# GpSimd takes 64 columns of each pair's exponential in a graph attention stage

## The chip, the cores and the metric

The kernel runs on one core of a Trainium2 chip. The metric is the device time of one execution in microseconds (us); the time before is the median of three runs. The engines are called PE (TensorE's matrix products; PEld its weight loads), DVE (VectorE), ACT (ScalarE), POOL (GpSimd) and SP (which issues most of the DMAs).

## The reference, cut to what matters

The reference is a graph network of four layers over 3327 nodes with 128 features and a dense 0/1 adjacency matrix. Each layer normalises `x`, applies a ReLU and adds its result to `x`. Nearly all of the time lies in layer 1, an attention in which each of 128 "heads" has only 8 features per node, and the adjacency matrix is added to the scores twice:

```python
q = (x @ Wq.T).reshape(d, n, h)        # d = 128 heads, n = 3327 nodes, h = 8
k = (x @ Wk.T).reshape(d, n, h)
v = (x @ Wv.T).reshape(d, n, h)
a = jnp.einsum('dnh,dmh->dnm', q, k) * scale
a = a + spatial_encoding + edge_encoding      # both are adj
a = jax.nn.softmax(a, axis=2)
out = jnp.einsum('dnm,dmh->dnh', a, v)
```

So for each of the 128 heads an array of 3327 x 3327 scores is made, 2*adj is added, the exponential is taken, and the result weighs the values. There are some 1.4 billion exponentials.

## The kernel before

The query nodes are cut into 7 chunks of columns, six of 476 and one of 471 (rounded up to 472 where an even width is needed). The heads are taken in 32 groups of four, and the 3327 keys in 26 tiles of up to 128. The loops run over chunks, then groups, then key tiles: 7 x 32 x 26 steps. Two neighbouring tiles, an even one and an odd one, make a **pair**, of which there are 7 x 32 x 13 = 2912. A pair has eight arrays of scores (four heads, two tiles) of 128 keys x 476 queries, held in one SBUF buffer `p8` with eight places. There are three such buffers in turn.

The order of the stage is written out by hand (`manual_schedule`); each engine works through its own queue in the order in which the program issues the instructions. A pair goes like this:

- PE makes the four products of the even tile into four PSUM banks `early` (L551), and DVE adds 2*adj (`a2`) to each and writes the sums to places 0 to 3 (L554).
- For the odd tile PE makes three products into a PSUM tile `late` and the fourth into an `early` bank. DVE adds `a2` to the fourth and writes it to place 4: this is the fifth sum of the pair. To one of the three late arrays PE itself adds `a2`, by a product with twice the identity (L570).
- ACT takes the exponential of the three late arrays into places 5 to 7 (L572), and then that of the five sums, in place (L575).
- Two of the late arrays haven't had `a2` added. For them POOL multiplies the exponentials by exp(2*adj), which is kept as `e_a` (L574). Where POOL has other work, this is one array rather than two, and PE adds to two: that is for the first five pairs of the first 30 groups of the first chunk, in which POOL also parts the queries and keys of a coming group into high and low halves (L376, L377).
- The exponentials weigh the values in products that follow four steps, or two pairs, behind (L582); after the last tile DVE copies the result (L591) and it is stored.

Between these, once a pair, a strided copy of two key tiles is made for the next group (`key_pair`, L426): on DVE right after the fifth add, but for one pair in a group on POOL. POOL also doubles the adjacency tiles of the next chunk (`doubled`, L273), 26 of them over the 32 groups of a chunk, and clears one column of `k_in` (L395) in each group.

```python
PLACES = ((0, 1, 2, 3), (5, 6, 7, 4))
...
scores(step, pairs, q4, a_t[t], e_t[t // 2], p8, 1 if parting and t < 10 else 2)
begun[j] = (step, v4, p8)
if j >= ahead:
    weigh(*begun.pop(j - ahead))
```

Of the kernel before, what the change touches and what calls it, by code (L numbers as in the profile page):

```python
# [1 line left out]

# [6 lines left out]
F32 = mybir.dt.float32  # L9
# [6 lines left out]
AF = mybir.ActivationFunctionType  # L16
ALU = mybir.AluOpType
# [4 lines left out]
P = 128  # L22
# [9 lines left out]
QW = 476  # L32
# [5 lines left out]
def rows_of(t):  # L38
    return P if t < T - 1 else P - 1
# [15 lines left out]
def kernel(  # L55
# [23 lines left out]
    nc = tc.nc  # L79

    const = ctx.enter_context(tc.tile_pool(name="const", bufs=1))
# [89 lines left out]
    def load_rows(dst, src, t, col0, w):  # L171

        def part(p0, p1):
            nc.sync.dma_start(dst[p0:p1, :w], dram(src, (p0 * T + t) * N + col0, [[T * N, p1 - p0], [1, w]]))

        if t < T - 1:
            part(0, P)
        else:
            part(0, 112)
            part(112, P - 1)  # L180
# [161 lines left out]
    def even(c):  # L342
        w = q_chunks[c][1]
        return w + w % 2

    def exp_of(a2, c):
        e = e_pool.tile([P, QW], F32, name="e")
        nc.scalar.activation(e[:, : even(c)], a2[:, : even(c)], AF.Exp)
        return e
# [72 lines left out]
    def key_pair(engine, k_in, pairs):  # L422

        t = 2 * len(pairs)
        k = kq.tile([P, 2, P], F32R, name="k", bufs=T // 2 + 2)
        engine.tensor_copy(k, slots(k_in)[:, t : t + 2, :])  # L426
        pairs.append(k)
# [84 lines left out]

    assert T % 2 == 0
    PLACES = ((0, 1, 2, 3), (5, 6, 7, 4))
    two_i = const.tile([P, P], BF16, name="two_i")
    nc.vector.tensor_copy(two_i, ident)
    engines = {
# [9 lines left out]
    with tc.tile_pool(name="at_in", bufs=1) as a_pool, tc.tile_pool(name="at_p", bufs=3) as p_pool, tc.tile_pool(  # L527
        name="at_ps", bufs=1, space=PSUM
    ) as ps:
        acc = ps.tile([P, 512], F32, name="acc")  # L530
        nc.vector.memset(acc, 0.0)

        def load_adj(c, t):

            q0, w = q_chunks[c]
            a = a_pool.tile([P, QW], F32, name="a_in", bufs=1)
            load_rows(a, adjT, t, q0, w)
            return a, t, w

        def store_adj(c, t, a2):  # L540
            q0, w = q_chunks[c]
            nc.sync.dma_start(adj16[t][:, q0 : q0 + w], a2[:, :w])

        def scores(step, pairs, q4, a2, e_a, p8, n_g):
            c, _, t = step
            we = even(c)
            k = pairs[t // 2]

            def product(i, sp, stop=True):
                r = slice(32 * i, 32 * i + 32)  # L550
                nc.tensor.matmul(sp[:, :we], k[r, t % 2, :], q4[r, :we], start=True, stop=stop)  # L551

            def add(i, sp):
                nc.vector.tensor_tensor(p8[:, PLACES[t % 2][i], :we], sp[:, :we], a2[:, :we], op=ALU.add)  # L554

            if t % 2 == 0:
                early = [ps.tile([P, 512], F32, name="early", bufs=4) for _ in range(4)]
                for i in range(4):
                    product(i, early[i])
                for i in range(4):  # L560
                    add(i, early[i])
                return
            n_i = 3 - n_g
            late = ps.tile([P, 3, 512], F32, name="late")
            early = ps.tile([P, 512], F32, name="early", bufs=4)
            for i in range(3):
                product(i, late[:, i], stop=i >= n_i)
            product(3, early)
            for i in range(n_i):
                nc.tensor.matmul(late[:, i, :we], two_i, a2[:, :we], start=False, stop=True)  # L570
            add(3, early)
            nc.scalar.activation(p8[:, 5:8, :we], late[:, :, :we], AF.Exp)  # L572
            g8 = p8[:, 8 - n_g : 8, :we]
            nc.gpsimd.tensor_tensor(g8, g8, e_a[:, :we].unsqueeze(1).to_broadcast([P, n_g, we]), op=ALU.mult)  # L574
            nc.scalar.activation(p8[:, :5, :we], p8[:, :5, :we], AF.Exp)  # L575

        def weigh(step, v4, p8):
            c, g, t = step
            q0, w = q_chunks[c]
            kp = rows_of(t)  # L580
            for i in range(4):
                nc.tensor.matmul(  # L582
                    acc[32 * i : 32 * i + EA, :w],
                    v4[:kp, i, t, :],
                    p8[:kp, PLACES[t % 2][i], :w],
                    start=(t == 0),
                    stop=(t == T - 1),
                )
            if t == T - 1:
                o4 = a_pool.tile([P, QW], F32, name="o4")  # L590
                nc.vector.tensor_copy(o4[: 96 + EA, :w], acc[: 96 + EA, :w])  # L591
                for i in range(4):
                    n0 = (4 * g + i) * N + q0
                    nc.sync.dma_start(ot[:, n0 : n0 + w], o4[32 * i : 32 * i + EA, :w])

        with tc.manual_schedule(engines=engines):
            groups = [(c, g) for c in range(len(q_chunks)) for g in range(n_groups)]
            steps = [(c, g, t) for c, g in groups for t in range(T)]
            (q4, v4), pairs = first, k_first
            a_t, a_next = a_first, []  # L600
            e_t, e_next = e_first, []
            to_store = [(0, t, a2) for t, a2 in enumerate(a_t)]
            begun = {}
            for j, step in enumerate(steps):
                c, g, t = step
                n = c * n_groups + g + 1
                more = n < len(groups)
                if t == 0:
                    if j:
                        (q4, v4), pairs = coming, k_coming  # L610
                        if g == 0:
                            a_t, a_next = a_next, []
                            e_t, e_next = e_next, []
                    k_coming = []
                if t % 2 == 0:
                    p8 = p_pool.tile([P, 8, QW], F32, name="p8")
                parting = c == 0 and g + 2 < n_groups
                scores(step, pairs, q4, a_t[t], e_t[t // 2], p8, 1 if parting and t < 10 else 2)
                begun[j] = (step, v4, p8)
                if j >= ahead:  # L620
                    weigh(*begun.pop(j - ahead))
                if t == 4 and more:
                    coming = load_rest(*groups[n])
                if parting:
                    if t == 0:
                        part = ahead_part
                    for due in range(t, t + 1 if t < T - 1 else max(T, 16)):
                        part.at(due)
                        if due == 15 and g + 3 < n_groups:
                            ahead_part = Parting(g + 3)  # L630
                            ahead_part.load(0)
                            ahead_part.load(1)

                if t % 2 and more:
                    key_pair(nc.gpsimd if t == ahead - 1 else nc.vector, k_ins[n], k_coming)
                if t == 14 and n + 1 < len(groups):
                    k_ins.append(load_keys(groups[n + 1][1]))
                if t == min(6, T // 2) and c + 1 < len(q_chunks):
                    for _ in range(min(len(to_store), 1 + T // n_groups)):
                        store_adj(*to_store.pop(0))  # L640
                    a_in = [load_adj(c + 1, i) for i in range(len(a_next), T * (g + 1) // n_groups)]
                if t == max(T - 4, 3) and c + 1 < len(q_chunks):
                    for a, i, w in a_in:
                        a_next.append(doubled(adj_pools[(c + 1) % 2], a[: rows_of(i), :w], i, w))
                        to_store.append((c + 1, i, a_next[-1]))
                if t % 2 and g == n_groups - 1 and c + 1 < len(q_chunks):
                    e_next.append(exp_of(a_next[t], c + 1))
            for j in range(len(steps) - ahead, len(steps)):
                weigh(*begun.pop(j))
            for a in to_store:  # L650
                store_adj(*a)
# [374 lines left out]
    with tc.For_i(0, n_once, 1):  # L1026
# [28 lines left out]
        with tc.tile_pool(name="gb", bufs=2) as pool, tc.tile_pool(name="gb_ps", bufs=2, space=PSUM) as ps, tc.tile_pool(  # L1055
            name="gb_acc", bufs=1, space=PSUM
# [3 lines left out]
            with tc.For_i(0, NH // 4, 1) as g:  # L1060
# [8 lines left out]
                for q0, w in chunks(N, QW):  # L1069
                    q4 = pool.tile([P, QW], F32, name="gq4")  # L1070
# [64 lines left out]
```

## Time and profile before

| | us |
|---|---|
| median of 3 runs | 11047.67 (11043.29 to 11047.72) |
| the profiled execution | 11044.8 |
| its span, first to last instruction | 11043.1 |
| mean granted TensorE clock | 0.988 |
| DVE busy | 10416.8 |
| ACT busy | 10027.8 |
| POOL busy | 7228.9 |

The first exponential of a pair starts at 590 us and the last one ends at 10315 us, so the attention stage has 88% of the span. "Busy" is the time in which at least one instruction of the engine is under way. Instructions of one engine overlap at their ends, so what one adds to its engine's time is the distance from its start to the next one's start, and not its duration. A group line of the profile reads: source line, engine, operation, names of output and inputs, shapes and types, count, then the busy time, the mean ns of one, the idle time before, and what ended it.

### The profile page before, as it was taken

The numbers are of one execution on the slowest core, as the hardware profiler recorded it, in microseconds if no ns is written. First come the engines' busy times: TensorE is split into PE (matmuls) and PEld (weight loads), VectorE is DVE, ScalarE is ACT, GpSimd is POOL, SyncE is SP. The second block draws the span as 40 slices with busy tenths as digits, with TensorE's granted clock in tenths as the row PEclk, the third lists the DMA queues.
The fourth block names the chain that finished last, engine by engine and source line by source line (L and its number), as shares of the span: only waits on it lengthen the run. The fifth ranks groups of instructions, "written<-read, shape, count | busy, mean of one in ns | idle before, by whom it ended". The sixth has DMA issues, their size and how long they took to land. (4 is left out here: it accounts for less than half of the span.)

```text
span 11043.1 us, 201872 instructions
## 1 busy us (share of the span) xinstructions
PE 10674.7 (97%) x76743; PEld 3215.5 (29%) x76768; DVE 10416.8 (94%) x18105; ACT 10027.8 (91%) x6240; POOL 7228.9 (65%) x4288
## 2 busy tenths in 40 slices
PE   9799999999999999999999999999999999999896
PEld 4322222222222222222222222222222222222453
DVE  8599999999999999999999999999999999999656
ACT  0399999999999999999999999999999999999432
POOL 0278887777777777777777777777777766666203
PEclk9899999999999999999999999999999999999998
DMA  7755555333333333333333333333333333333432
GB/s 264 228 142 127 123 124 120 63 67 68 63 70 65 62 71 64 65 69 63 65 71 63 66 69 62 69 65 62 69 64 62 72 58 60 60 56 64 139 106 99
DMA packets 417648, 943.48 MB, mean 85 GB/s; under 512 B 67952, under 2 KB 345953, under 8 KB 380956
## 3 DMA queue, kind: packets, MB, share of 16 engines
q1 hardware_dynamic: 412906, 920.68, 38.9%
q8 instruction: 606, 9.93, 0.4%
q0 software_dynamic: 3760, 9.78, 0.3%
q14 instruction: 376, 3.08, 0.1%
HBM read 790.49 MB, written 139.71 MB: 84 GB/s over the span
## 5 line engine op out<-in xcount | busy, mean ns | idle before, releaser
L554 DVE TENSOR_TENSOR p<-early,a 128x476 f32<-128x476 f32 (+1 forms) x14560 | 8409.7, 645 | 115.7 <-PE early L551 90.1
L574 POOL TENSOR_TENSOR p<-p,e 128x952 f32<-128x952 f32 (+2 forms) x2912 | 6333.2, 2175 | 2690.2 <-ACT p L572 2285.3
L575 ACT ACTIVATE p<-p 128x2380 f32<-128x2380 f32 (+1 forms) x2912 | 7424.2, 2550 | 0.0
L582 PE MATMUL acc<-p,v 128*9 128x476 f32 (+1 forms) x46592 | 5736.5, 564 | 50.8 <-issue 35.0
L572 ACT ACTIVATE p<-late 128x1428 f32<-128x1428 f32 (+1 forms) x2912 | 4998.2, 1716 | 13.9 <-DMA q<-qt 10.3
L551 PE MATMUL early<-q,k 32*128 32x476 f32 (+1 forms) x14560 | 3682.7, 478 | 29.9 <-DVE p L554 7.5
L551 PEld LDWEIGHTS early<-q,k 32*128 32x128 f32 x14560 | 1578.3, 182 | 2725.5 <-DVE p L554 2702.2
L426 DVE CAST k<-k_in 128x256 fp32r<-128x256 f32 x2676 | 1467.7, 548 | 0.0
L551 PE MATMUL late<-q,k 32*128 32x476 f32 (+1 forms) x8736 | 1416.6, 479 | 49.5 <-ACT p L572 49.3
L551 PEld LDWEIGHTS late<-q,k 32*128 32x128 f32 x8736 | 548.5, 182 | 2371.9 <-ACT p L572 2204.6
L570 PE MATMUL late<-a,two_i 128*128 128x476 bf16 (+1 forms) x3062 | 1122.5, 375 | 0.0
L582 PEld LDWEIGHTS acc<-p,v 128*9 128x9 f32 x46592 | 702.1, 89 | 1363.5 <-issue 1288.5
L570 PEld LDWEIGHTS <-two_i 128*128 128x128 bf16 x3062 | 281.3, 96 | 662.7 <-issue 662.7
L190 ACT COPY agg<-agg_ps 128x512 f32<-128x512 f32 x15 | 8.2, 591 | 486.6 <-PE agg_ps L205 290.1
L273 POOL TENSOR_SCALAR a<-a_in 128x476 bf16<-128x476 f32 (+2 forms) x156 | 239.4, 1535 | 0.5
L231 PE MATMUL agg_ps<-a,part 128*128 128x512 bf16 (+1 forms) x1067 | 227.8, 371 | 6.2 <-ACT agg L953 3.2
L273 POOL TENSOR_SCALAR a<-a 128x476 bf16<-128x476 f32 (+1 forms) x26 | 36.4, 1400 | 287.8 <-DMA a<-in_adjT_dram 287.8
L426 POOL CAST k<-k_in 128x256 fp32r<-128x256 f32 x236 | 175.2, 746 | 12.5 <-DMA q<-qt 12.5
L948 PE MATMUL sp<-yT,hT 128*128 128x512 f32 (+1 forms) x364 | 171.3, 612 | 11.6 <-ACT agg L953 5.7
L205 PE MATMUL agg_ps<-a,h 128*128 128x512 f32 (+2 forms) x364 | 147.7, 569 | 26.2 <-DVE h L165 26.2
L591 DVE COPY o<-acc 105x476 f32<-105x476 f32 (+1 forms) x224 | 145.9, 651 | 12.0 <-PE acc L582 7.0
L864 POOL TENSOR_TENSOR xs_late<-xs_late,b_s 128x3328 f32<-128x3328 f32 x1 | 7.3, 7268 | 225.2 <-DVE ln_xc L160 225.2
(239 smaller groups left out, 2860.9 us busy)
## 6 DMA issues: line engine op xcount, KB each, us to landing
k_in<-kt SPq DMA_DIRECT2D x1792, 207.9 KB
v<-vd SPq DMA_DIRECT2D x896, 117.0 KB
a<-in_adjT_dram SPq DMA_DIRECT2D x50, 1663.5 KB
a<-adj SPq DMA_DIRECT2D x78, 831.8 KB
q<-qt SPq DMA_DIRECT2D x1536, 29.8 KB
a_in<-in_adjT_dram SPq DMA_DIRECT2D x125, 238.0 KB
adj<-a SPq DMA_DIRECT2D x156, 119.0 KB
vd<-v_st SPq DMA_DIRECT2D x25, 576.0 KB
```

Of the source, the lines that this page charges most:

```text
L205: nc.tensor.matmul(acc[c][:, :w], lhs[:kp, t, :], a[:kp, c0 : c0 + w], start=(t == 0), stop=(t == T - 1))
L231: nc.tensor.matmul(acc[c][:, :w], part[:, t, :], a[:, c0 : c0 + w], start=(t == 0 and i == 0), stop=(t == T - 1 and i == len(parts) - 1),)
L273: nc.gpsimd.tensor_scalar(a2[:kp, :w], a, 2.0, None, op0=ALU.mult)
L426: engine.tensor_copy(k, slots(k_in)[:, t : t + 2, :])
L551: nc.tensor.matmul(sp[:, :we], k[r, t % 2, :], q4[r, :we], start=True, stop=stop)
L554: nc.vector.tensor_tensor(p8[:, PLACES[t % 2][i], :we], sp[:, :we], a2[:, :we], op=ALU.add)
L570: nc.tensor.matmul(late[:, i, :we], two_i, a2[:, :we], start=False, stop=True)
L572: nc.scalar.activation(p8[:, 5:8, :we], late[:, :, :we], AF.Exp)
L574: nc.gpsimd.tensor_tensor(g8, g8, e_a[:, :we].unsqueeze(1).to_broadcast([P, n_g, we]), op=ALU.mult)
L575: nc.scalar.activation(p8[:, :5, :we], p8[:, :5, :we], AF.Exp)
L582: nc.tensor.matmul(acc[32 * i : 32 * i + EA, :w], v4[:kp, i, t, :], p8[:kp, PLACES[t % 2][i], :w], start=(t == 0), stop=(t == T - 1),)
L948: nc.tensor.matmul(sp[:, c0 : c0 + w], slots(zT)[:, t, :], z2T[:, cols], start=True, stop=False)
```

## The change

In every pair but those in which POOL parts queries and keys, POOL raises e to the last 64 columns of the fifth sum, in place, by a `tensor_tensor` with the operation `pow`, whose first operand is a column of e read for every element. It stands in POOL's queue just ahead of the pair's multiply. ACT's second exponential leaves these 64 columns out: it reads 5 x 476 - 64 = 2316 columns (2296 in the last chunk) rather than 2380 (2360). For that, the places of `p8` now lie next to each other in the last chunk too, with 472 columns each rather than 476.

```diff
+    W_POW = 64
+    base = const.tile([P, 1], F32, name="base")
+    nc.vector.memset(base, math.e)
...
-        def scores(step, pairs, q4, a2, e_a, p8, n_g):
+        def scores(step, pairs, q4, a2, e_a, p8, n_g, w_pow):
...
-            nc.scalar.activation(p8[:, 5:8, :we], late[:, :, :we], AF.Exp)
-            g8 = p8[:, 8 - n_g : 8, :we]
+            nc.scalar.activation(p8[:, 5:8], late[:, :, :we], AF.Exp)
+            flat = p8.rearrange("p i w -> p (i w)")
+            if w_pow:
+                last = flat[:, 5 * we - w_pow : 5 * we]
+                nc.gpsimd.tensor_tensor(last, base.to_broadcast([P, w_pow]), last, op=ALU.pow)
+            g8 = p8[:, 8 - n_g : 8]
             nc.gpsimd.tensor_tensor(g8, g8, e_a[:, :we].unsqueeze(1).to_broadcast([P, n_g, we]), op=ALU.mult)
-            nc.scalar.activation(p8[:, :5, :we], p8[:, :5, :we], AF.Exp)
+            sums = flat[:, : 5 * we - w_pow]
+            nc.scalar.activation(sums, sums, AF.Exp)
...
-                    p8 = p_pool.tile([P, 8, QW], F32, name="p8")
+                    p8 = p_pool.tile([P, 8 * QW], F32, name="p8")[:, : 8 * even(c)].rearrange("p (i w) -> p i w", i=8)
                 parting = c == 0 and g + 2 < n_groups
-                scores(step, pairs, q4, a_t[t], e_t[t // 2], p8, 1 if parting and t < 10 else 2)
+                parts_now = parting and t < 10
+                scores(step, pairs, q4, a_t[t], e_t[t // 2], p8, 1 if parts_now else 2, 0 if parts_now else W_POW)
```

More of the change, by code (lines that the diff above doesn't have):

```diff
@@ L1 @@
+import math
 from contextlib import ExitStack
```

## The prediction

> **What bounds the kernel now.** I read four views: the engine shares, the table of stretches, the costliest groups, and the timelines of ScalarE, GpSimd and VectorE over the same microseconds. The chain that ended last never leaves the final stage here, so it can't name the bound of the attention stage; the table of stretches can. First the shares, then a stretch inside that stage (its columns are PE, weight loads, DVE, ACT, POOL, granted clock, DMA share, GB/s).
>
> ```profile
> PE 10674.7 (97%) x76743; PEld 3215.5 (29%) x76768; DVE 10416.8 (94%) x18105; ACT 10027.8 (91%) x6240; POOL 7228.9 (65%) x4288
> ```
> ```profile
> 5000.00:6400.00 1400.00, 1379.81 (x10480) 377.12 (x10483) 1381.63 (x2515) 1400.00 (x853) 996.91 (x510) 1.00 0.35 67
> ```
>
> ScalarE is busy for all 1400 us; PE and DVE look nearly as full, POOL is at 71%. The groups give the work of one pair of key tiles (2912 pairs): five adds (L554) on DVE, one multiply (L574) on POOL, two exponentials (L572, L575) on ACT.
>
> ```profile
> L554 DVE TENSOR_TENSOR p<-early,a 128x476 f32<-128x476 f32 (+1 forms) x14560 | 8409.7, 645 | 115.7 <-PE early L551 90.1
> L574 POOL TENSOR_TENSOR p<-p,e 128x952 f32<-128x952 f32 (+2 forms) x2912 | 6333.2, 2175 | 2690.2 <-ACT p L572 2285.3
> L575 ACT ACTIVATE p<-p 128x2380 f32<-128x2380 f32 (+1 forms) x2912 | 7424.2, 2550 | 0.0
> L572 ACT ACTIVATE p<-late 128x1428 f32<-128x1428 f32 (+1 forms) x2912 | 4998.2, 1716 | 13.9 <-DMA q<-qt 10.3
> ```
>
> Busy shares hide overlap and stalls, so I use distances between starts. ScalarE's timeline:
>
> ```profile
> 5625.05 2.53 ACT L575 ACTIVATE p<-p 128x2380 f32<-128x2380 f32 x1
> 5627.12 1.70 ACT L572 ACTIVATE p<-late 128x1428 f32<-128x1428 f32 x1
> 5628.36 2.54 ACT L575 ACTIVATE p<-p 128x2380 f32<-128x2380 f32 x1
> 5630.44 1.71 ACT L572 ACTIVATE p<-late 128x1428 f32<-128x1428 f32 x1
> 5631.68 2.54 ACT L575 ACTIVATE p<-p 128x2380 f32<-128x2380 f32 x1
> ```
>
> L575 takes 2.08 us and L572 1.24, 3.32 a pair, without a gap: ScalarE sets the period. The extra columns of L575 cost (2.08 - 1.24)/(2380 - 1428) = 0.88 ns each. Over a whole chunk of columns (416 pairs) the timeline puts the first L572 at 1992.59 and the next chunk's at 3382.29: 3.341 us a pair with everything in it. In the last chunk it is 3.299. Now GpSimd and VectorE, where one doubling (L273) falls:
>
> ```profile
> 5628.90 2.23 POOL L574 TENSOR_TENSOR p<-p,e 128x952 f32<-128x952 f32 x1 [1.10 <-ACT p L572]
> 5631.10 1.57 POOL L273 TENSOR_SCALAR a<-a_in 128x476 bf16<-128x476 f32 x1
> 5632.64 2.22 POOL L574 TENSOR_TENSOR p<-p,e 128x952 f32<-128x952 f32 x1
> 5635.55 2.23 POOL L574 TENSOR_TENSOR p<-p,e 128x952 f32<-128x952 f32 x1 [0.69 <-ACT p L572]
> ```
> ```profile
> 5624.43 0.39 DVE L426 CAST k<-k_in 128x256 fp32r<-128x256 f32 x1
> 5624.74 2.88 DVE L554 TENSOR_TENSOR p<-early,a 128x476 f32<-128x476 f32 x5
> ...
> 5631.32 2.87 DVE L554 TENSOR_TENSOR p<-early,a 128x476 f32<-128x476 f32 x5
> 5634.12 1.01 DVE L426 CAST k<-k_in 128x256 fp32r<-128x256 f32 x1
> 5635.06 1.21 DVE L554 TENSOR_TENSOR p<-early,a 128x476 f32<-128x476 f32 x2
> ```
>
> Two things. Five adds take 2.80 us (5631.32 to 5634.12), a free key cast 0.31; with the copy of a group's results that is 3.15 a pair, so DVE has about 0.17 to spare. And the cast that begins while POOL multiplies lasts until 5635.13, 0.27 after the multiply's end (5634.86): it can't run beside a POOL multiply. The idle 1.10 us of POOL is thus partly the cast's place. The reverse shows in POOL's own casts, 0.42 at the median and up to 0.62 where they come after a held-up DVE cast: 0.20 lost to POOL.
>
> ```profile
> L376 POOL CAST hi<-lo_q x128: 404/419/624, 395.5 to 1874.3; 96x278 fp32r<-96x278 f32 x96, 96x275 fp32r<-96x275 f32 x32
> L395 POOL MEMSET k_in<- 128x1 f32 x224 | 22.9, 103 | 0.0
> ```
>
> **The change, part by part.** The power runs wherever POOL has no parting work: 2912 pairs less 5 in each of 30 groups, 2762.
>
> *ScalarE, less.* 64 columns x 0.88 ns = 56 ns, times 2762 = 155 us, all of it on the path as long as ScalarE sets the period. The Trainium skill ("ScalarE: Activation LUTs", Rules for kernel authors) calls ScalarE the only option for an exponential; by that rule nothing would be moved, and the sum would be the time of before.
>
> *Next late.* DVE at 3.15 and PE, whose pair takes 3.10 where nothing holds it (early products start at 5002.62 and 5005.72), are both under the new 3.27, so neither takes the 56 ns away while casts stay free.
>
> *GpSimd, more: the unknown.* No row shows a power. From below: the two-input multiply, (2230 - 1205)/476 = 2.15 ns a column between its 952- and 476-column forms and 0.18 us fixed, so 0.18 + 64 x 2.15 ns = 0.32 us; nothing can be below that row by much, since the power too reads two operands and writes one, and a negative cost is excluded because an instruction is added to POOL and none taken away. From above: a power is a logarithm and an exponential. With a cubic for each (three multiply-adds), a step that splits off the exponent and one that puts it back, I count ten operations beyond what a multiply does, and twice that for a careful version. One operation costs at most a whole one-input pass: the cast row, (0.419 - 0.103)/277 = 1.14 ns a column with its read and write, 0.073 us for 64. Ten make 0.32 + 0.73 = 1.05 us, twenty 1.78. Between 0.32 and 1.78 I take 1.05: by what it computes the power is nearer to a chain of passes than to one multiply. By the Trainium skill ("GPSIMD Engine Reference", section 3.1), loop bodies of three or more operations run about three a cycle at 1.2 GHz; ten would add about 0.18 us, the power would be an estimated 0.50 us and the change would gain; no trace here shows that rate.
>
> *The new wait.* The power waits for DVE's fifth add, and stands ahead of the same pair's multiply in POOL's queue; behind it are that multiply, a key cast per group, the doubling and the memset of k_in. DVE issues its key cast right after the fifth add, so the cast goes first and the power comes after it. A power that fits between the cast and the end of L572 delays nothing; a longer one pushes the multiply, the multiply holds the next cast, and POOL closes a loop: cast, power, multiply. The weighing products of the odd tile now need the power too, but they already wait for the multiply behind it and stand two pairs later. The multiply starts 1.10 us after the last, so the cover is 1.10 less the cast's 0.20 and the small work.
>
> *POOL's loop.* A group has 13 pairs: 13 multiplies at 2.20 (5628.90 to 5631.10), 13 x 0.20 for casts, one key cast of 0.69, 0.81 doublings (26 in 32 groups) at 1.54, 0.10 of memset: 33.2, or 2.56 a pair without the power. With a power of X the pair takes 2.56 + X. That meets today's 3.341 at X = 0.78, and ScalarE's shortened 3.285 at 0.73. In the last chunk (no doublings, 2.19 a multiply) it is 2.46 + X against 3.299, level at 0.84.
>
> *The sum.* X = 1.05: (3.61 - 3.341) x 2346 pairs = 631, (3.51 - 3.299) x 416 = 88, together +719 us; ScalarE's 155 is then idle time. The profiled execution took 11044.8 (span 11043.1 and 1.7 around it), which gives 11764; the median of the runs is 2.9 above it: 11767. Ends of this case: X = 0.80 gives +45 (2346 pairs at +0.019; the last chunk stays with ScalarE), X = 1.78 gives +2735 (0.999 x 2346 + 0.941 x 416). New starts: one memset of 128x1, 0.1 us, on DVE beside other work. That p8 is packed in the last chunk costs nothing: there L575 with gaps runs at 2.06 us for 2360 columns, the same per column.
>
> **The rivals.**
> *Faster.* The power overlaps its arithmetic with its reads and stays near the multiply, X under 0.73; ScalarE remains the bound. For: same instruction and type as L574, and 1.10 us of idle POOL in front of each multiply. Against: it must compute a logarithm. Price: -155 us, of which a group's doubling takes some back: POOL then needs 1.54 + 0.20 + 0.32 + 2.20 = 4.26 in a period of 3.27, so the cast waits about 0.4 longer than now; with half of it reaching ScalarE, 0.2 x 156 doublings = 31 us, and by the same reckoning some 10 for the key casts. Time 10935, from 10893 (nothing taken back) to 11020. It decides for X below 0.78.
> *Far slower.* The power is worked in a long dependent chain or lane by lane, X over 1.78: POOL is the bound from the first pair, each further microsecond costs 2762 us; at X = 3 it is 17150. For: nothing in the trace shows POOL doing anything but single operations. Against: no elementwise POOL row costs over 3.3 ns a column (L273: 1.57 us for 476).
> *No change.* X between 0.73 and 0.78, or below that with all casts held (2.80 + 0.50 = 3.30 on DVE): within 22 us of 11048.
>
> **How the numbers follow.** POOL's loop as the bound with X from 0.79 to 1.78: 0.42, the likeliest, 11767, its own range 11070 to 13780. Faster 0.36, no change 0.05, far slower 0.17. The range 10890 to 13780 leaves out the far slower case, and some 0.02 at the ends of the others. Measurements of this kernel can tell 0.2%, 22 us, from no change; slower is 0.42 + 0.17 = 0.59.
>
> **What would show it.** Right: the power's group near 1 us, POOL near 100% in the stretches of the attention stage, ScalarE under 93%, multiplies that start when the power ends rather than when L572 does, casts at 0.6 and more. Wrong: POOL still idle before the power with ScalarE at 100% (the faster case), or a power beyond 1.8 us. If DVE were full with free casts, my 3.15 would be wrong.

## The result, and the profile after

The changed kernel takes **37072.11 us** (median; 37071.26 to 37076.38) against 11045.69 for the kernel before beside it: a ratio of 3.3564, 95% interval 3.3505 to 3.3622. The profiled execution took 37071.85, its span 37070.1, its mean granted TensorE clock 0.681.

First the engine shares of the changed kernel, then the rows of its 40 slices for PE, POOL and the granted clock:

```profile
PE 18306.6 (49%) x76768; PEld 3481.3 (9%) x76768; DVE 10369.7 (28%) x18106; ACT 10176.0 (27%) x6240; POOL 35925.1 (97%) x7050
```
```profile
PE   7555544444444444444444444444444444444447
POOL 4999999999999999999999999999999999999993
PEclk8777666666666666666666666666666666666668
```

GpSimd has gone from 65% of a short span to 97% of a long one, and ScalarE from 91% to 27%. One stretch inside the attention stage (PE, weight loads, DVE, ACT, POOL, granted clock, DMA share, GB/s) confirms it: POOL is busy in every microsecond of 2000, each other engine in half of them or fewer.

```profile
5000.00:7000.00 2000.00, 946.22 (x3904) 155.88 (x3906) 512.85 (x936) 530.07 (x314) 2000.00 (x349) 0.67 0.09 17
```

The groups name the instruction (line, engine, operation, shapes, count, then busy time, mean ns of one, idle time before):

```profile
L580 POOL TENSOR_TENSOR p<-base,p 128x64 f32<-128x64 f32 x2762 | 29135.8, 10549 | 1.6 <-DVE p L558 1.6
L591 PE MATMUL acc<-p,v 128*9 128x476 f32 (+1 forms) x46592 | 12755.0, 895 | 18533.1 <-POOL p L582 16874.8
L558 DVE TENSOR_TENSOR p<-early,a 128x476 f32<-128x476 f32 (+1 forms) x14560 | 8558.6, 646 | 24189.5 <-PE early L555 24112.0
L582 POOL TENSOR_TENSOR p<-p,e 128x952 f32<-128x952 f32 (+2 forms) x2912 | 6273.7, 2155 | 27.1 <-ACT p L576 26.6
L584 ACT ACTIVATE p<-p 128x2316 f32<-128x2316 f32 (+2 forms) x2912 | 6188.2, 2125 | 0.0
```

One power on 64 columns takes 10.5 us, with almost no idle time before it. GpSimd's timeline, two pairs long, gives the whole period:

```profile
15005.41 2.37 POOL L582 TENSOR_TENSOR p<-p,e 128x952 f32<-128x952 f32 x1
15007.55 10.71 POOL L580 TENSOR_TENSOR p<-base,p 128x64 f32<-128x64 f32 x1
15018.04 2.37 POOL L582 TENSOR_TENSOR p<-p,e 128x952 f32<-128x952 f32 x1
15020.19 10.71 POOL L580 TENSOR_TENSOR p<-base,p 128x64 f32<-128x64 f32 x1
```

2.14 us from multiply to power, 10.49 from power to multiply, 12.63 together. With the doublings, POOL's own key casts and the memset the mean over a chunk is 12.77 us a pair in the second to sixth chunks and 12.645 in the last, against 3.341 and 3.299 before. The table of waits, read alone, would blame PE (engine and line, what it waited for, total us, times, longest):

```profile
ACT p L576 <- PE late L574: 25150.1, 2688, 12.6
DVE p L558 <- PE early L555: 24112.0, 2674, 11.8
PEld acc L591 <- POOL p L582: 19266.4, 2514, 10.9
```

ScalarE and VectorE wait for PE's products, but PE stands in its queue at the weighing products, and these wait for POOL's multiply, which stands behind the power. Each of those waits has to be followed back to the engine that doesn't wait. PE's own slowness is no part of the cause: its clock fell to 0.67 here and a weighing product took 895 ns, yet PE was idle half of the time.

### The profile page after: what moved, and what is told of

Read it like the earlier page. It is cut to its first block, busy times and chain, and to the rows that moved or that the text cites. A ratio compares the mean times of both kernels' runs of the same rounds, so it can differ in the third digit from the quotient of the medians.

```text
span 37070.1 us, 204465 instructions
## 1 busy us (share of the span) xinstructions
PE 18306.6 (49%) x76768; PEld 3481.3 (9%) x76768; DVE 10369.7 (28%) x18106; ACT 10176.0 (27%) x6240; POOL 35925.1 (97%) x7050
## 5 line engine op out<-in xcount | busy, mean ns | idle before, releaser
L580 POOL TENSOR_TENSOR p<-base,p 128x64 f32<-128x64 f32 x2762 | 29135.8, 10549 | 1.6 <-DVE p L558 1.6
L591 PE MATMUL acc<-p,v 128*9 128x476 f32 (+1 forms) x46592 | 12755.0, 895 | 18533.1 <-POOL p L582 16874.8
L576 ACT ACTIVATE p<-late 128x1428 f32<-128x1428 f32 (+1 forms) x2912 | 3956.6, 1359 | 25175.4 <-PE late L574 25150.1
L584 ACT ACTIVATE p<-p 128x2316 f32<-128x2316 f32 (+2 forms) x2912 | 6188.2, 2125 | 0.0
L555 PE MATMUL early<-q,k 32*128 32x476 f32 (+1 forms) x14560 | 4080.6, 723 | 13.9 <-DVE p L558 9.7
L591 PEld LDWEIGHTS acc<-p,v 128*9 128x9 f32 x46592 | 1009.0, 94 | 23195.8 <-POOL p L582 19266.4
L555 PE MATMUL late<-q,k 32*128 32x476 f32 (+1 forms) x8736 | 1864.8, 633 | 0.2 <-ACT p L576 0.2
L574 PE MATMUL late<-a,two_i 128*128 128x476 bf16 (+1 forms) x3062 | 1354.5, 451 | 0.0
L555 PEld LDWEIGHTS late<-q,k 32*128 32x128 f32 x8736 | 727.1, 243 | 4245.7 <-issue 4101.4
L427 DVE CAST k<-k_in 128x256 fp32r<-128x256 f32 x2676 | 1083.7, 405 | 0.4
```

What stands on the lines that cost most here:

```text
L576: nc.scalar.activation(p8[:, 5:8], late[:, :, :we], AF.Exp)
L580: nc.gpsimd.tensor_tensor(last, base.to_broadcast([P, w_pow]), last, op=ALU.pow)
L584: nc.scalar.activation(sums, sums, AF.Exp)
L591: nc.tensor.matmul(acc[32 * i : 32 * i + EA, :w], v4[:kp, i, t, :], p8[:kp, PLACES[t % 2][i], :w], start=(t == 0), stop=(t == T - 1),)
```

## The experiments

Each kernel is the changed one with the edit shown. Where a time has a ratio, it is the ratio to the kernel before, with its 95% interval; the others were run once.

**1. The saving alone.** The power is gone, ScalarE's second exponential is still 64 columns shorter; these columns stay plain sums.

```diff
-                nc.gpsimd.tensor_tensor(last, base.to_broadcast([P, w_pow]), last, op=ALU.pow)
+                pass
```

> The change without its power: ScalarE still leaves the 64 columns out and nobody raises them (those columns of the fifth array stay plain sums). Theory (the power alone is slow; ScalarE bounds the kernel without it): the period falls by 64 x 0.88 ns = 56 ns in 2762 pairs, 155 us, to about 10892. Rival (something else of the change is slow: the packed places, the shorter exponential): well over 11048, towards 37000. Rival (DVE or PE is level with ScalarE already): no change, 11048.

Measured: 10926.76, ratio 0.9896 (0.9881 to 0.9911). A stretch of it:

```profile
5000.00:7000.00 2000.00, 1983.52 (x15188) 542.68 (x15187) 1961.78 (x3646) 1998.84 (x1229) 1440.07 (x741) 1.00 0.35 67
```

ScalarE is still full. The saving is real but is 116 us, not 155. A pair is shorter by 52 ns at the median (3.266), by 45 in the mean of the second to sixth chunks (3.295; from the first pair's start to the last one's, so counted, it was 3.340 before) and by only 11 in the first (3.359), where 266 of the 416 pairs are shortened. With 64 columns in this kernel, a POOL instruction that cost nothing would bring this.

**2. The instruction with cheap arithmetic.** Same operands, place and waits, but an add.

```diff
-                nc.gpsimd.tensor_tensor(last, base.to_broadcast([P, w_pow]), last, op=ALU.pow)
+                nc.gpsimd.tensor_tensor(last, base.to_broadcast([P, w_pow]), last, op=ALU.add)
```

> The power's operation is replaced by an addition: same instruction, operands, place in the queue and 64 columns (the columns become e plus the sum). Theory (only the power's arithmetic is slow): the instruction takes about 0.32 us by the multiply's rate, POOL keeps idle time, and the time is the 10935 that the prediction gave for a cheap power (10893 to 11020). Rival (an instruction more in POOL's queue with a wait for DVE is what costs): 11100 or more, POOL full.

Measured: 10980.19, ratio 0.9944 (0.993 to 0.9957).

```profile
L580 POOL TENSOR_TENSOR p<-base,p 128x64 f32<-128x64 f32 x2762 | 952.2, 345 | 1283.8 <-DVE p L558 1254.3 <-DVE k L427 15.0 <-POOL p L582 0.2
```

With 0.345 us in place of 10.549 the kernel gains. So the new wait, the queue order and the broadcast operand aren't what costs 26,000 us; the operation `pow` itself is. The add has a price all the same: 53 us against experiment 1. After the first chunk the two kernels have the same period; in the first chunk the add's is 3.481 against 3.359, and 416 pairs x 0.122 = 51 us. A stretch of that chunk, the add first, then the kernel without it:

```profile
700.00:1900.00 1200.00, 1172.85 (x8764) 309.36 (x8756) 1159.50 (x2073) 1152.25 (x691) 1008.55 (x1052) 0.98 0.52 120
```
```profile
700.00:1900.00 1200.00, 1192.02 (x9106) 315.77 (x9105) 1171.90 (x2154) 1192.35 (x719) 975.27 (x870) 1.00 0.53 124
```

**3. The same add, not in the first chunk.** The first chunk is the one in which POOL also parts queries and keys for a coming group.

```diff
-                scores(step, pairs, q4, a_t[t], e_t[t // 2], p8, 1 if parts_now else 2, 0 if parts_now else W_POW)
+                scores(step, pairs, q4, a_t[t], e_t[t // 2], p8, 1 if parts_now else 2, 0 if c == 0 else W_POW)
```

(with the add in place of the power)

> The addition in place of the power, in chunks 1 to 6 alone; chunk 0 is as before. Theory (what the addition cost over the shorter exponential alone, 53 us, lies in chunk 0, where POOL also parts queries and keys: its period there was 3.481 against 3.359): chunks 1 to 6 keep a period of 3.295, time 11043 - 0.045 x 2080 - 0.040 x 416 = 10933. Rival (the loss is spread over all chunks): 10980 or more.

Measured: 10932.12, ratio 0.9899 (0.9883 to 0.9914), as expected. The add's loss lies in the first chunk, and the trace of experiment 2 shows where in it. In 10 of the first 30 groups the seventh and eighth pairs take 4.4 to 6.3 us each; these ten groups are 46 us longer than in experiment 1. Each of the ten has one VectorE key cast of 3.4 us, and experiment 1 has none over 1.7. One of them, between POOL's instructions:

```profile
833.35 2.23 POOL L582 TENSOR_TENSOR p<-p,e 128x952 f32<-128x952 f32 x1
834.84 3.40 DVE L427 CAST k<-k_in 128x256 fp32r<-128x256 f32 x1
835.53 0.29 POOL L580 TENSOR_TENSOR p<-base,p 128x64 f32<-128x64 f32 x1
835.78 2.21 POOL L582 TENSOR_TENSOR p<-p,e 128x952 f32<-128x952 f32 x1
```

POOL comes late from the parting work, so multiply, add and multiply follow one another without a gap. The cast begins in the first multiply and ends at 838.24, 0.25 after the second one; VectorE's next sums wait for it, and PE stands idle for 2.07 us. The granted clock is then 0.70 and 0.62 in the two stretches of 5 us from 839 to 849. Why the cast isn't released between the two multiplies is left open.

**4. Half the columns.** If the cost is per column, half of them take half the time.

```diff
-    W_POW = 64
+    W_POW = 32
```

> The power on 32 columns rather than 64. Theory (cost by the column: 0.18 us fixed and 10.34/64 = 0.16 us a column): 5.35 us for one power, pair 2.25 + 5.35 = 7.60 us, time about 22800. Rival (a large fixed cost per power, such as a call or a code load, and cheap columns): one power still over 9 us, time over 33000.

Measured: 23241.94 (one run), 2% over what was expected.

```profile
L580 POOL TENSOR_TENSOR p<-base,p 128x32 f32<-128x32 f32 x2762 | 15185.3, 5498 | 0.2 <-DVE p L558 0.2
```

From the power's start to POOL's next start it is 5.38 us at the median, against 10.49 for 64 columns: (10.49 - 5.38)/32 = 0.16 us a column.

**5. and 6. Four columns and two.** These ask for the fixed part, and whether any width pays.

```diff
-    W_POW = 64
+    W_POW = 4
```

> The power on 4 columns. Theory (0.16 us a column): 0.83 us for one. By the prediction's loop (2.56 + X a pair) that is 3.39, slower than ScalarE's 3.33: about 11160. Rival (the casts run beside the power, so the loop is 2.25 + X = 3.08): ScalarE stays the bound, about 11040, no change that can be measured. Rival (large fixed cost per power): over 30000.

Measured: 11441.69, ratio 1.0361 (1.0347 to 1.0375). The groups of the power and of VectorE's key casts, and a stretch:

```profile
L580 POOL TENSOR_TENSOR p<-base,p 128x4 f32<-128x4 f32 x2762 | 3171.3, 1148 | 13.6 <-DVE p L558 9.2 <-POOL p L582 2.2
...
L427 DVE CAST k<-k_in 128x256 fp32r<-128x256 f32 x2676 | 1993.5, 745 | 0.0
```
```profile
2200.00:5000.00 2800.00, 2734.93 (x20102) 741.33 (x20102) 2786.95 (x4827) 2728.28 (x1634) 2790.35 (x1786) 1.00 0.33 64
```

This kernel happens to have the power that I forecast for 64 columns (about 1 us), so it shows the forecast's world. POOL is full, and the distances between its starts add up to the period of 3.483 us: 2.19 for the multiply, 1.13 for the power, 0.17 for the rest. ScalarE isn't full. DVE looks full too, because its key casts, 0.745 us each in place of 0.40 in the changed kernel, are held by POOL's multiplies. The two engines hold each other up: a power of four columns takes 0.97 from its start to the next start, but 1.16 where a held cast is still under way when it begins. With neither held up POOL's sum would be some 3.28 (an estimate: 2.145 + 0.975 + the prediction's 0.16 for key cast, doublings and memset), under ScalarE's 3.32. It was slower than expected because I had the fixed part at 0.18 us. Now the line through 64, 32 and 4 columns could be drawn: 0.35 us and about 0.16 for each column. It was put to use for two:

```diff
-    W_POW = 64
+    W_POW = 2
```

> The power on 2 columns. From the three widths (10.49, 5.38 and 0.975 us from its start to the next instruction's at 64, 32 and 4 columns) it takes 0.35 + 2 x 0.157 = 0.66 us. Theory (POOL's loop, level with ScalarE at a power of 0.78 us): under the level, ScalarE stays the bound in chunks 1 to 6; the period there is 3.33 to 3.34, and the first chunk, where POOL parts queries and keys, loses some 50 us as it did with the addition: about 11090. Rival (any power this long hurts, for the casts it holds up): the excess of pow4 (398 us) falls only with the columns, to some 11250 or more. Rival (a gain from two columns): 11040 or less.

Measured: 11090.55, ratio 1.0042 (1.0028 to 1.0056). The total is as expected, in part by luck: the first chunk lost 28 us and not 50, and the second to sixth lost 22 that weren't expected (3.348 to 3.355 a pair; before: 3.340). The power takes at least 0.65 from start to start. Two columns save ScalarE 2 x 0.88 = 1.8 ns a pair, 5 us in all, and the kernel is 46 us slower. None of the four widths pays.

```profile
L580 POOL TENSOR_TENSOR p<-base,p 128x2 f32<-128x2 f32 x2762 | 2110.0, 764 | 435.8 <-DVE p L558 406.1 <-DVE k L427 8.6 <-POOL k_in L396 0.2
```

**7. Eight lanes of 128.** One of the reasons that I gave for a dear power was that it is worked lane by lane.

```diff
-                nc.gpsimd.tensor_tensor(last, base.to_broadcast([P, w_pow]), last, op=ALU.pow)
+                nc.gpsimd.tensor_tensor(last[:8], base[:8].to_broadcast([8, w_pow]), last[:8], op=ALU.pow)
```

> The 64-column power on partitions 0 to 7 alone (the others keep plain sums), so that one of POOL's cores works on 8 rows and the rest on none. Theory (the cores take a whole column of 16 rows at a time, by a long routine): one power stays at 10.5 us and the time near 37000. Rival (lane by lane, as the prediction's third case put it): half the rows, about 5.4 us for one, time about 23200.

Measured: 37071.01 (one run).

```profile
L580 POOL TENSOR_TENSOR p<-base,p 8x64 f32<-8x64 f32 x2762 | 29046.7, 10517 | 1.2 <-DVE p L558 1.2
```

A sixteenth of the elements, the same 10.5 us: the price is for a column, with 8 partitions as with 128. "Lane by lane" is refuted in the sense of the expectation, by which half the rows take half the time; a routine that goes over all lanes, used or not, would look the same.

**8. Easy numbers.** A power with a branch on its values might be dear for e and cheap for a base of 1.

```diff
-    nc.vector.memset(base, math.e)
+    nc.vector.memset(base, 1.0)
```

> The base of the power is 1 rather than e, so that every result is 1 and the logarithm 0; 64 columns. Theory (a routine of fixed length per column, whatever the numbers): 10.5 us for one power, 37070. Rival (the routine is long because of these numbers, with a short way for simple ones): well below 10 us.

Measured: 37073.69 (one run), 10.543 us a power. The base makes no difference, and over the 2762 powers of the changed kernel, on different sums each, the duration stays between 10.51 and 10.72.

```profile
L580 POOL TENSOR_TENSOR p<-base,p 128x64 f32<-128x64 f32 x2762 | 29121.0, 10543 | 1.4 <-DVE p L558 1.4
```

**9. Another place in the queue.** 32 columns, with the power behind the pair's multiply.

```diff
+            g8 = p8[:, 8 - n_g : 8]
+            nc.gpsimd.tensor_tensor(g8, g8, e_a[:, :we].unsqueeze(1).to_broadcast([P, n_g, we]), op=ALU.mult)
             if w_pow:
                 last = flat[:, 5 * we - w_pow : 5 * we]
                 nc.gpsimd.tensor_tensor(last, base.to_broadcast([P, w_pow]), last, op=ALU.pow)
-            g8 = p8[:, 8 - n_g : 8]
-            nc.gpsimd.tensor_tensor(g8, g8, e_a[:, :we].unsqueeze(1).to_broadcast([P, n_g, we]), op=ALU.mult)
```

> The power on 32 columns stands behind the pair's multiply in POOL's queue rather than ahead of it. Theory (POOL's loop is the sum of its instructions, in whatever order): the time of the 32-column power ahead of the multiply, 23242, within 1%. Rival (the power's place, ahead of the multiply that the weighing and the casts wait for, is what costs): a clear part of the 12200 us between 23242 and 11045 comes back.

Measured: 23020.41 (one run), 1% less than experiment 4, as expected. An engine that is full for the whole stage has nearly the same work in either order.

```profile
L582 POOL TENSOR_TENSOR p<-base,p 128x32 f32<-128x32 f32 x2762 | 15557.7, 5633 | 0.0
```

**10. What relieving ScalarE can bring at most.** No power, and ScalarE's second exponential shorter by 240 columns, which stay plain sums.

```diff
-    W_POW = 64
+    W_POW = 240
...
-                nc.gpsimd.tensor_tensor(last, base.to_broadcast([P, w_pow]), last, op=ALU.pow)
+                pass
```

> No power, and ScalarE leaves out 240 columns of the fifth array rather than 64 (they stay plain sums). ScalarE's pair would be 3.32 - 240 x 0.82 ns = 3.12 us. Theory (DVE at 3.15 and PE at 3.10 are next): a period of about 3.17 in chunks 1 to 6, time about 10600. Rival (DVE or PE are level with ScalarE at 3.27 already, since casts are held up): 10900, as with 64 columns.

Measured: 10912.68, ratio 0.9881 (0.9866 to 0.9896); the rival was right and I was wrong. With 240 x 0.88 = 211 ns taken from ScalarE the mean period is 3.290 (second to sixth chunks), where 64 columns gave 3.295. A stretch, then VectorE's timeline in it, then PE's even products and one of their weight loads:

```profile
5000.00:7000.00 2000.00, 1986.44 (x15205) 544.55 (x15208) 1958.08 (x3649) 1953.96 (x1230) 1441.00 (x743) 1.00 0.35 66
```
```profile
5002.79 0.40 DVE L427 CAST k<-k_in 128x256 fp32r<-128x256 f32 x1
5003.14 2.90 DVE L558 TENSOR_TENSOR p<-early,a 128x476 f32<-128x476 f32 x5
5005.95 0.41 DVE L427 CAST k<-k_in 128x256 fp32r<-128x256 f32 x1
5006.51 2.90 DVE L558 TENSOR_TENSOR p<-early,a 128x476 f32<-128x476 f32 x5
```
```profile
5002.53 0.88 PE L555 MATMUL early<-q,k 32*128 32x476 f32 x4
5002.93 0.18 PEld L555 LDWEIGHTS early<-q,k 32*128 32x128 f32 x1 [0.21 <-DVE p L558]
5005.90 0.68 PE L555 MATMUL early<-q,k 32*128 32x476 f32 x4
```

ScalarE isn't full any more (98%), and neither is VectorE (98%), whose casts are mostly free here. PE's busy share is 99%, but its pair isn't always the same. Pairs alternate: early products start at 5002.53, 5005.90 and 5009.06, so one pair takes 3.37 and the next 3.16. In the first PE waits 0.21 for VectorE to empty the last of the four early banks, and its four products take 0.88 rather than 0.68. In the second VectorE waits for PE's early products (from cast to adds it is 0.35 at 5002.79, where nothing holds them, and 0.56 at 5005.95). The exchange through these banks is next late, at about 3.27 to 3.29 a pair, and no busy share shows it. In the last chunk 64 and 240 columns give the same 3.26 a pair. The reading rests on these waits; no run gave the exchange more banks. The table of waits is no help: PE's weight loads wait 2608 us for VectorE here and 2702 in the kernel before, mostly while PE itself is busy with weighing products.

## Why the prediction was wrong

Slower was right, and so was the mechanism, POOL's queue as a loop that sets the period, but for the cast that the prediction put in that loop; the size was not: 11767 us forecast, 37072 measured, outside the range of 10890 to 13780. Point by point:

- **The power's cost X: the step that failed.** "By what it computes the power is nearer to a chain of passes than to one multiply": so I took 1.05 us, between 0.32 and 1.78; it is 10.49. I had counted ten operations and priced each at a whole one-input pass, 1.14 ns a column; the measured slope of 0.16 us a column is 140 such passes. The error is in the upper bound: a count of arithmetic in my head, at a rate from POOL's simple operations, was used as if it bounded a row that the trace doesn't have.
- **POOL's loop.** Put X = 10.49 into the prediction's own sum, and it gives (2.56 + 10.49 - 3.341) x 2346 + (2.46 + 10.49 - 3.299) x 416 = 26,790, so some 37,840 us: 2% above the 37,072. Most of that rest of 768 us is the 0.20 that I charged in each pair for a held cast (0.20 x 2762 = 552); here the casts fall into the power, run freely in it, as the last section shows, and take 0.40, not the 0.6 and more that I named as a sign. Another 152 is the multiply, 2.145 from start to start where I had 2.20. At four columns, where casts are held, the loop was closer: 2.56 + 0.97 = 3.53 for 3.483 measured.
- **"Far slower".** This was the case that came, with X over 1.78, and its price was right in kind: each further microsecond costs 2762 us. I gave it 0.17. Of its two reasons, "lane by lane" is refuted in the sense of experiment 7; the "long dependent chain" is neither shown nor excluded. The argument against it, that no elementwise POOL row costs over 3.3 ns a column, said nothing of an operation that no row contains.
- **ScalarE's saving.** 155 us forecast, 116 measured. The 56 ns a pair came out as 52 at the median. In the second to sixth chunks all the loss is in the second pair of a group, in which VectorE also copies the last group's result: it takes 3.42 us where it took 3.35, and the other twelve save 54 ns in the mean. The doublings, to which I gave 31 us, cost nothing that shows (3.287 us in their pairs and 3.297 elsewhere, and with the add 3.287 and 3.298).
- **What is next late.** VectorE at 3.15 and PE at 3.10 were no floor: experiment 10 stays near 3.29, though ScalarE's pair was to be 3.12. I had added each engine's free work and left out the handing over of banks between the two. Had the power been as cheap as the add, the "Faster" case would still have been about right (10935, its range to 11020; the add gave 10980), but by luck: what was lost went at the second pair of each group and in the first chunk, not at the doublings that most of it was put down to.
- **The rule on ScalarE.** The Trainium skill ("ScalarE: Activation LUTs", Rules for kernel authors) would have left the exponential where it was, and the runs agree with it as to time: on ScalarE a column costs 0.88 ns, by POOL's power 160.
- **The rule on GpSimd.** The rate in "GPSIMD Engine Reference", section 3.1 gave an estimate of 0.50 us for the power; the measurement, 10.49, decides against it by a factor of 21. Whether that rate or my count of ten operations is what fails, no run shows. The two-input multiplies of this case, 2.15 ns a column, agree with the 2.6 cycles that the same section gives.

## What to carry to other kernels

A row that the trace doesn't have can't be bounded from above by counting the arithmetic that it "must" do; before work goes to another engine, time one instruction of exactly that operation there, at two widths, and the slope and the fixed part settle the matter. Compare that slope with the one that is saved: here 160 ns a column was to replace 0.88, and neither a smaller width nor the other place that was run mended that. And what an engine's relief is worth at most can be had by itself, by leaving the work out: here 116 us for 64 columns and about 132 for 240.

## What the runs showed of the hardware that I had not expected

GpSimd's elementwise power in fp32 costs 0.16 us a column and about 0.35 fixed; at 64 columns it costs the same for 8 and for 128 partitions and for either base.

A VectorE key cast that begins in a POOL multiply lasts until about 0.27 after that multiply's end, in the kernel before and in nearly all cases in those with narrower powers. Beside a power of 64 columns it doesn't: all 2555 casts of the changed kernel that began in a power, 2.9 to 6.4 us after its start and with over 4 us of it left, took 0.40. Both cases in one timeline, of the kernel with 32 columns:

```profile
10003.24 2.20 POOL L582 TENSOR_TENSOR p<-p,e 128x952 f32<-128x952 f32 x1
10003.36 2.35 DVE L427 CAST k<-k_in 128x256 fp32r<-128x256 f32 x1
...
10005.39 5.60 POOL L580 TENSOR_TENSOR p<-base,p 128x32 f32<-128x32 f32 x1
...
10009.83 0.40 DVE L427 CAST k<-k_in 128x256 fp32r<-128x256 f32 x1
```

The first cast lasts to 10005.71, 0.27 after the multiply; the second, within the power, takes 0.40. "SBUF — State Buffer" (Who interferes with whom) in the Trainium skill describes a port shared by the two engines and held for a whole instruction: the multiply behaves so; the power doesn't, for most of its length. In this kernel of 32 columns 1183 of the 1625 casts that begin in the last 2 us of a power are held after all, and of the 120 that begin earlier one. With the power behind the multiply (experiment 9) only 105 of 748 in the last 2 us are. Why is left open.
